# GpSimd takes the first unit's second-level sums in one row, the down-projection folds go two chunks at a time, and VectorE's order at the end of phase 3 changes

## The chip, the cores and the metric

The kernel runs on one core of a Trainium2 chip. Its engines work side by side and wait for one another through semaphores: TensorE (PE in the profile, with its weight loads as PEld), VectorE (DVE), ScalarE (ACT), GpSimd (POOL), and SyncE (SP), which here only issues DMAs. The metric is the device time of one execution in microseconds (us); lower is better.

## The reference

One transformer layer with its two branches in parallel, in float32, on an input of 2 batches x 1024 tokens x 512 features:

```python
xn = layernorm(x)
# linear attention, 16 heads of 32
Q, K, V = elu(xn @ wq.T + bq) + 1, elu(xn @ wk.T + bk) + 1, xn @ wv.T + bv
KV, K_sum = sum_s K[s] V[s]^T, sum_s K[s]                 # for each head
attn = (Q KV / (Q . K_sum + 1e-8)) @ wo.T + bo
# feed-forward, 1376 hidden units, with low-rank terms of rank 8
w = top-2 of 8 experts by sigmoid(xn @ W_router) + bias, normalised scores
gate = xn @ W_gate + (xn @ sA_gate @ sB_gate + sum_e w_e xn @ A_gate[e] @ B_gate[e]) / 8
up   = likewise with W_up, sA_up, sB_up, A_up, B_up
hidden = silu(gate) * up
ffn = hidden @ W_down + (hidden @ sA_down @ sB_down + sum_e w_e hidden @ A_down[e] @ B_down[e]) / 8
out = x + attn + ffn
```

The shared low-rank factors (sA, sB) don't depend on the token, so the kernel adds their product to the weights ("folds" it in); the experts' terms are computed apart.

## The kernel before, in words

All products are done by a scheme of seven products for a 2x2 split (instead of eight), for which sums and differences of blocks of the weights and of the activations have to be made first. Engine order is written out by hand for PE, DVE, ACT and POOL: each runs its instructions in the order in which the program emits them. Only SP's order of DMA issues is chosen by the framework.

Phases 1 and 2 (to about 251 us of the span) normalise and transpose the tokens, make keys and queries, and store the scaled queries to memory. Phase 3 (251 to 532 us) makes the hidden units. Phase 4 (from 532 us) multiplies hidden units and queries with the down and the attention-output weights, in four units.

**Phase 3** consists of ten units `unit(j, b)`: pairs of 128-column weight chunks `j` = 0 to 4, each for batch `b` = 0 and 1. In a unit five of the seven outer products (numbers 1, 6, 2, 5 and 3) are themselves split by the seven-product scheme; each is an `Inner` object with steps `a`, `b`, `c`, `d` of matmuls of 128x256 (line 955) into two PSUM banks tagged `ab0/x0` or `ab1/x1`, copies by ACT (lines 965 to 988) and additions by DVE (`a_sum` line 969, `c_sum` line 983, `d_sum` line 991). Products 7 and 4 are plain 128x512 matmuls (line 1015) into banks `held2/held3`; low-rank terms (line 1010) go there and into `held0/held1`. DVE adds the products up (`add`, line 1037), ACT applies silu (line 1022), and a delayed list (`later`, `flush`) holds the multiplications h*up (line 1025) with their stores to `h_dram`. `unit` has named places (`at("6c")`, `at("1d")` and so on) where the caller hooks other work in.

For an inner product, second-level sums are needed: of the weights (`inner_weight_sums`, lines 930 to 933; `p` names the outer product, 1, 5 and 6 together as 128x384, 2 and 3 alone as 128x128) and of the tokens (`token_sums_56` and `token_sums_23` through line 886 as 128x512, `token_sums_1` lines 908 to 911 as 128x256; four operations each). Weight sums are made for each j, token sums once for each batch. `token_diffs` (line 1251) makes `xdiff0` and `xdiff1`, read by the low-rank matmuls late in every unit. `u4 = r5 + u2` in each unit is two POOL additions of 128x512.

Before the change, DVE makes the token sums of batch 1 and p = 1, 5, 6 inside `unit(0, 0)` and the weight sums of p = 2 just ahead of it; POOL makes `ti23_0` near the end of phase 2, then the weight sums of p = 3, `xdiff`, u4, and `ti23_1`.

**Folding the down weights** (`fold_down`): for each pair of 128-row chunks of `W_down` (`wd[j]`, chunks j and j + 5), two matmuls with 8 rows of contraction (line 1178) multiply the low-rank factors into two banks `x0`, `x1`; DVE adds them to the weights (line 1182, 128x512 each), and POOL makes four block differences (lines 1144 to 1147). The 8 rows lie in one of four groups of 32 partitions, `rows = slice(i % SG * 32, ...)` with i = 8 + chunk and SG = 4. The same is done in the units for the gate and up weights (`fold_pe`, line 716), there with four matmuls of 8x256 at a time. In `unit(4, 0)` and `unit(4, 1)` five such pairs and the rest `wdr` are folded, one pair at a time.

**The end of phase 3**: behind its last `d` step, PE goes straight into phase 4's `products(0, ...)`: for each of seven accumulators two matmuls of 128x256 (line 1383). Those take the banks ab0, ab1, x0, x1, then held0, held1, held2; held0 and held1 are first read out by `add(V, u4, u4, py)`. Chunk n = 1 needs `feature_sums(0, 1)` (lines 1267 to 1270, four operations of 128x256 on DVE) from its third matmul on. The h tiles have three buffers (`hp`, bufs=3), so that the fourth silu of a unit waits for the store of the first h.

Of the kernel before, what the change touches and what calls it, by code (L numbers as in the profile page):

```python
# [37 lines left out]
def layer_kernel(  # L38
# [23 lines left out]
    nc = tc.nc  # L62
# [832 lines left out]

    def token_sums_56(b, t):
        yield from sums_of_four(nc.vector, tsum_pair[b], t)
        inner_tokens(b, (5, 6), lambda i, k: t[:, i, k])
# [4 lines left out]

    def token_sums_1(b):

        t = xnT[b][0][:, :, TB:BT].rearrange("p k (h n) -> p k h n", n=TH)
        b11, b21 = tsum[b][1][:, 0], tsum[b][1][:, 1]
        nc.vector.tensor_sub(t[:, 0, 0], b11[:, TH:], b11[:, 0:TH])
        nc.vector.tensor_sub(t[:, 0, 1], b21[:, TH:], t[:, 0, 0])
        nc.vector.tensor_sub(t[:, 1, 0], b21[:, TH:], b11[:, TH:])  # L910
        nc.vector.tensor_sub(t[:, 1, 1], b21[:, 0:TH], t[:, 0, 1])
        inner_tokens(b, (1,), lambda i, k: t[:, k // 2, k % 2])
# [34 lines left out]
    class Inner:  # L947


        def __init__(self, j, b, p, tag, n):  # L950
            self.w, self.t = WI[j, p], TI[b, p]
            self.n, self.name = n, f"{p}_{tag}"

        def mm(self, out, n, start=False):
            nc.tensor.matmul(out, self.w[n], self.t[n], start=start, stop=True, skip_group_check=True)  # L955

# [43 lines left out]
    def unit(j, b, hooks={}):  # L1000
# [43 lines left out]
        V, G = nc.vector, nc.gpsimd  # L1044
        late_x = b == 1 or j == NP - 1
        pb = [held(f"b{m}_{tag}", 2 + m) for m in range(2)]
# [85 lines left out]
        at("3d")  # L1132
        flush()
        add(V, u4, u4, py)
        r3 = i3.r
        add(V, r3, r3, u4)
# [26 lines left out]

    def fold_down(js, rest=False):

        to, pf = [], []

        def products():
            for j in js:
                for half in range(2):  # L1170
                    to.append((j + half * NP, wd[j][:, 2 * half : 2 * half + 2, :].rearrange("p s n -> p (s n)")))
            if rest:
                to.append((FULL, wdr[0:REST, :]))
            for f, v in to:
                i, n = 2 * NC + f, v.shape[0]
                rows = slice(i % SG * 32, i % SG * 32 + RANK)
                pf.append(spare_bank(f"x{len(pf)}", f"pfd{f}"))
                nc.tensor.matmul(pf[-1][0:n, :], sat[rows, i // SG, 0:n], sb_d[rows, :], start=True, stop=True)

        def sums():  # L1180
            for (f, v), p in zip(to, pf):
                nc.vector.tensor_add(v, v, p[0 : v.shape[0], :])
            for j in js:
                block_diffs(wd[j])
            if rest:
                for t, w in ((wdr_diff, wdr), (bd_diff, bd_sb)):
                    nc.gpsimd.tensor_sub(t, w[:, 0:HD], w[:, HD:D])

        return products, sums
# [34 lines left out]
    denominators(1)  # L1224
    list(token_sums_56(0, slot(6, [2, 4, TH], "ti56_0")))
    rest(0, (fold(0, 0), lambda: attend(1, 0)))
    attend(1, 1)
    list(token_sums_23(0, slot(4, [2, 4, TH], "ti23_0")))
    token_sums_1(0)
    rest(1, (fold(0, 1), lambda: list(inner_weight_sums(nc.vector, 0, (1, 5, 6)))))  # L1230
# [11 lines left out]
    ti56_1 = p3.tile([P, 2, 4, TH], F32, name="ti56_1")  # L1242
    list(inner_weight_sums(nc.vector, 0, (2,)))
    list(inner_weight_sums(nc.gpsimd, 0, (3,)))
    xdiff = []
# [19 lines left out]
    def feature_sums(u, i):  # L1265
# [4 lines left out]
        nc.vector.tensor_sub(t[:, 7, :], t[:, 2, :], t[:, 5, :])  # L1270

    def next_pair(j):

        pf = {}


        free = ("held0", "held1", "x0", "x1"), ("ab0", "x0", "ab1", "x1")

        def pe(i):
            return lambda: pf.update({i: fold_pe(j, i, free[i])})  # L1280

# [22 lines left out]
    for j in range(NP - 1):  # L1304
# [3 lines left out]
        if j == 0:  # L1308
            first["3b"] = [lambda: list(token_sums_23(1, slot(7, [2, 4, TH], "ti23_1")))]
            first["2c"] = [token_diffs]  # L1310
            sums1 = token_sums_56(1, ti56_1)
            for at in ("1d_sum", "6d_sum"):
                first[at] = [lambda: next(sums1, None)] * 2
            first["5b"] = [lambda: token_sums_1(1)]
            first["3d"] = [lambda: next(sums1, None)]
        unit(j, 0, first)
        unit(j, 1, second)
    load_down(1, 8)
    load_down(2, "t3")
    folds = [fold_down((j,)) for j in (1, 2, 0, 3, 4)]  # L1320
    fold_wdr = fold_down((), rest=True)
    unit(NP - 1, 0, {
        "6c": [folds[0][0]], "1d": [folds[0][1]], "5b": [folds[1][0]], "5c": [folds[1][1]],
        "3c": [fold_wdr[0]], "3d": [fold_wdr[1]],
    })
    load_down(0, 6)
    load_down(3, 0)
    load_down(4, 1)
    for i in range(3):
        load_feature(0, i)  # L1330
    unit(NP - 1, 1, {
        "6c": [folds[2][0]], "1d": [folds[2][1]], "2c": [folds[3][0]], "5c": [folds[3][1]],
        "3b": [lambda: feature_sums(0, 0)], "3c": [folds[4][0]], "3d": [folds[4][1]],
        "end": [lambda: feature_sums(0, 1), lambda: feature_sums(0, 2)],
    })
# [190 lines left out]
```

## Time and profile before

| | before |
|---|---|
| device time, median of 3 runs | 756.84 us (755.92 to 757.6) |
| the profiled execution, its own time | 756.2 us |
| its span, first to last instruction | 754.4 us |
| PE busy | 739.2 us (98%), 3106 instructions |
| DVE busy | 470.4 us (62%), 979 instructions |
| ACT busy | 201.1 us (27%) |
| POOL busy | 147.8 us (20%), 189 instructions |
| DMA | 63.29 MB, mean 84 GB/s |
| granted TensorE clock | 0.997 |

The profile shows each engine's busy intervals with the line of the kernel, the operation, its tiles and shapes. "x8" behind a line counts merged instructions, and a float32 matmul appears as two. A bracket at the end tells how long the engine had stood idle before that line, and who ended the wait. Start times count from the start of the span. L955 is line 955 of the kernel before; the changed file is one to six lines off from there.

### The profile page before, as it was taken

The page shows a single profiled execution, that of the slowest core. Times are in us where ns is not written, and L with a number is a line of the kernel's source. Part 1 is how long each engine was busy: PE and PEld are TensorE (multiplying, and loading weights), DVE is VectorE, ACT ScalarE, POOL GpSimd, SP SyncE. Part 2 cuts the span into 40 slices and gives each one's busy share as a digit, 9 for nine tenths or more (in the row PEclk, how much of TensorE's full clock was granted, in tenths as well). Part 3 has the DMA queues.
Part 4 walks back from the last instruction along what each step waited for, and adds up shares of the span by engine and source line. Part 5 has one row for each costly group of instructions (what it writes and reads, how often), then busy time and mean ns, then how long its engine had stood idle before and what let it go on. Part 6 is the DMA issues. An engine that isn't in the chain of part 4 may idle for free.

```text
span 754.4 us, 8739 instructions
## 1 busy us (share of the span) xinstructions
PE 739.2 (98%) x3106; PEld 496.8 (66%) x3106; DVE 470.4 (62%) x979; ACT 201.1 (27%) x432; POOL 147.8 (20%) x189
## 2 busy tenths in 40 slices
PE   8999999999999999999999999999899999999997
PEld 6666666454333566566666666656688888888886
DVE  5666665455677888888888879777942602603303
ACT  3545352533433233333343343333000000000000
POOL 3211212012000541312213114144701002201001
PEclk9999999999999999999999999999999999999999
DMA  8701001007314001211210301353555407312001
GB/s 244 215 28 43 15 0 57 0 1 190 113 29 136 22 4 56 83 53 37 84 57 29 112 29 56 112 167 111 168 161 173 146 10 239 125 60 109 28 1 56
DMA packets 52733, 63.29 MB, mean 84 GB/s; under 512 B 9425, under 2 KB 39505, under 8 KB 52434
## 3 DMA queue, kind: packets, MB, share of 16 engines
q1 hardware_dynamic: 52018, 62.46, 26.0%
q8 instruction: 24, 0.39, 0.2%
q10 hardware_dynamic: 672, 0.28, 0.2%
q14 instruction: 19, 0.16, 0.1%
HBM read 40.97 MB, written 21.76 MB: 83 GB/s over the span
## 4 chain that ended last, share of the span: by engine, by line
PE 83%; DVE 11%; ACT 2%; issue 2%; DMA 1%; POOL 0%; DVEq 0%; SPq 0%; ACTq 0%; POOLq 0%
PE po L1383 24%; PE ab L955 13%; PE pk L279 7%; PE pg L307 6%; PE b L1015 6%; PE pqu L559 3%; PE ph L1406 3%; DVE r L1037 2%; PE x L955 2%; PE pqv L559 2%; PE pxa L638 2%; PE b L1010 2%; PE pr L850 2%; PE x L1010 1%; DVE t L1037 1%
## 5 line engine op out<-in xcount | busy, mean ns | idle before, releaser
L1383 PE MATMUL po<-wd,f 128*128 128x256 f32 x560 | 123.1, 380 | 2.5 <-DVE f L1269 1.2
L1383 PEld LDWEIGHTS po<-wd,f 128*128 128x128 f32 x560 | 105.8, 190 | 19.4 <-issue 2.1
L1015 PE MATMUL b<-t,w 128*128 128x512 f32 x160 | 83.2, 601 | 0.0
L279 PE MATMUL pk<-wk_sb,xnT 128*128 128x256 f32 (+1 forms) x256 | 61.0, 392 | 1.4 <-ACT xnT L267 1.4
L307 PE MATMUL pg<-kt,xn 128*128 128x512 f32 x128 | 57.5, 592 | 0.0
L1413 DVE TENSOR_TENSOR had<-ph,wT 64x256 f32<-64x256 f32 x8 | 3.4, 422 | 86.0 <-PE ph L1406 85.9
L279 PEld LDWEIGHTS pk<-wk_sb,xnT 128*128 128x128 f32 x256 | 48.4, 194 | 9.3 <-ACT xnT L267 2.1
L1430 ACT COPY a<-po 128x512 f32<-128x512 f32 x4 | 2.3, 585 | 195.7 <-PE po L1383 195.7
L1383 PE MATMUL po<-kvo,f 128*128 128x256 f32 x224 | 49.4, 381 | 0.0
L1037 POOL TENSOR_TENSOR r<-r,r 128x512 f32<-128x512 f32 x20 | 30.3, 1537 | 87.7 <-DVE t L1037 87.7
L1383 PEld LDWEIGHTS po<-kvo,f 128*128 128x128 f32 x224 | 42.2, 190 | 7.1 <-issue 1.2
L955 PE MATMUL ab<-ti,wi 128*128 128x256 f32 x180 | 45.7, 380 | 0.0
L955 PEld LDWEIGHTS ab<-ti,w 128*128 128x128 f32 x140 | 25.2, 189 | 30.0 <-DVE r L983 9.1
L955 PEld LDWEIGHTS ab<-ti,wi 128*128 128x128 f32 x180 | 34.1, 190 | 13.9 <-issue 5.3
L955 PE MATMUL ab<-ti,w 128*128 128x256 f32 x140 | 41.1, 387 | 1.1 <-DVE r L983 0.8
L1037 DVE TENSOR_TENSOR r<-r,r 128x512 f32<-128x512 f32 x60 | 41.2, 726 | 0.0
L307 PEld LDWEIGHTS pg<-kt,xn 128*128 128x128 f32 x128 | 24.3, 190 | 25.2 <-issue 23.7
L988 ACT COPY r<-ab 128x256 f32<-128x256 f32 x50 | 18.6, 372 | 76.3 <-PE ab L955 76.3
L1015 PEld LDWEIGHTS b<-t,w 128*128 128x128 f32 x160 | 29.2, 190 | 10.9 <-issue 6.6
L305 POOL TENSOR_TENSOR ksum<-ksum,kt 128x512 f32<-128x512 f32 x14 | 19.9, 1423 | 78.4 <-DVE kt L297 47.7
L983 DVE TENSOR_TENSOR r<-r,ab 128x256 f32<-128x256 f32 x50 | 20.5, 415 | 18.4 <-ACT r L980 17.8
L991 DVE TENSOR_TENSOR r<-r,ab 128x256 f32<-128x256 f32 x50 | 20.8, 417 | 16.9 <-ACT r L988 16.7
(234 smaller groups left out, 1257.7 us busy)
## 6 DMA issues: line engine op xcount, KB each, us to landing
h_dram<-h SPq DMA_DIRECT2D x40, 256.0 KB
f<-h_dram SPq DMA_DIRECT2D x20, 512.0 KB
x_ring<-in_x_dram SPq DMA_DIRECT2D x16, 256.0 KB
q_dram<-qt SPq DMA_DIRECT2D x16, 256.0 KB
f<-q_dram SPq DMA_DIRECT2D x8, 512.0 KB
xr<-in_x_dram SPq DMA_DIRECT2D x8, 512.0 KB
out_dram<-xr SPq DMA_DIRECT2D x16, 256.0 KB
w<-in_w_gate_dram SPq DMA_DIRECT2D x10, 256.0 KB
```

What stands on the lines that cost most here:

```text
L279: nc.tensor.matmul(pk[s], xt(i // TPBATCH, c, cols), wk_sb[:, c, s * HD : (s + 1) * HD + s * E], start=(c == 0), stop=(c == NC - 1),)
L305: nc.gpsimd.tensor_add(ksum, ksum, kt)
L307: nc.tensor.matmul(pg[m], xn[:, ts(m, P)], kt, start=(j == 0), stop=(j == TPBATCH - 1))
L559: nc.tensor.matmul(banks[c], wqs[p][:, k, ts(c, P)], tsum[b][p][:, k, :], start=(start and k == 0), stop=(k == 1), skip_group_check=True,)
L955: nc.tensor.matmul(out, self.w[n], self.t[n], start=start, stop=True, skip_group_check=True)
L983: nc.vector.tensor_add(self.r[1][:, H1], self.r[1][:, H1], self.lo)
L991: nc.vector.tensor_add(self.r[1][:, H0], self.r[1][:, H0], self.lo)
L1010: nc.tensor.matmul(banks[m], bgu_sb[rows, cols], act[rows, :], start=starts[m], stop=True, skip_group_check=True)
L1015: nc.tensor.matmul(pb[m], ws[m][:, A_OF[p], ts(k, P)], tsum[b][p][:, k, :], start=start, stop=True, skip_group_check=True)
L1037: eng.tensor_add(to[m], t[m], v[m])
L1383: nc.tensor.matmul(ps[p][:, q, :], lhsT, rhs, start=start, stop=stop, skip_group_check=True)
L1406: nc.tensor.matmul(ph[g * ER : (g + 1) * ER, :], a, f[:, g, :], start=(n == 0), stop=(n == len(chunks) - 1), skip_group_check=True,)
```

## The change

1. **The first unit's sums.** The DVE operations for the second-level sums of p = 2 weights (j = 0), `ti56_1`, and `token_sums_1` of batch 1 go to POOL, and `ti23_0`, which POOL made in phase 2, moves behind them. All of POOL's sums then stand in one row ahead of unit (0, 0): weights p = 2, weights p = 3, `ti23_0`, `token_sums_1(1)`, `ti56_1`, `ti23_1`, and behind them `xdiff` and u4 of unit (0, 0). An inner product looks its operands up when it emits a matmul, since they are registered later.
2. **Folds of down.** Chunks 1 and 3 are folded together at "6c" of unit (4, 0), chunks 0 and 2 together at "6c" of unit (4, 1), with the banks held0, held1, x0, x1; chunk 4 as before; the rest `wdr` at "6d" of unit (4, 0). Chunk 3 takes the `t3` buffer and chunk 2 the slot that was chunk 3's. In unit (4, 0), `u1 += px` stands behind i5's `c_sum` instead of ahead of i2's `b`.
3. **DVE's order at the end of phase 3.** In unit (4, 1) the two delayed h multiplications no longer stand ahead of `u4 += py`, but behind the feature sums; `feature_sums(0, 1)` comes between `u4 += py` and `r3 += u4`.

On SP one order changes: the second load for chunk 4 goes behind two h stores of unit (4, 0).

```diff
@@ -893,22 +893,22 @@
             TI[b, p] = {1: raw[:, 0, 0:TH], 2: raw[:, 1, 0:TH], 3: raw[:, 1, TH:TB],
                         4: t(i, 3), 5: t(i, 0), 6: t(i, 1), 7: t(i, 2)}
 
-    def token_sums_56(b, t):
-        yield from sums_of_four(nc.vector, tsum_pair[b], t)
+    def token_sums_56(eng, b, t):
+        yield from sums_of_four(eng, tsum_pair[b], t)
         inner_tokens(b, (5, 6), lambda i, k: t[:, i, k])
 
     def token_sums_23(b, t):
         yield from sums_of_four(nc.gpsimd, xnT[b][1].rearrange("p k (g n) -> p g k n", g=2), t)
         inner_tokens(b, (2, 3), lambda i, k: t[:, i, k])
 
-    def token_sums_1(b):
+    def token_sums_1(eng, b):
 
         t = xnT[b][0][:, :, TB:BT].rearrange("p k (h n) -> p k h n", n=TH)
         b11, b21 = tsum[b][1][:, 0], tsum[b][1][:, 1]
-        nc.vector.tensor_sub(t[:, 0, 0], b11[:, TH:], b11[:, 0:TH])
-        nc.vector.tensor_sub(t[:, 0, 1], b21[:, TH:], t[:, 0, 0])
-        nc.vector.tensor_sub(t[:, 1, 0], b21[:, TH:], b11[:, TH:])
-        nc.vector.tensor_sub(t[:, 1, 1], b21[:, 0:TH], t[:, 0, 1])
+        eng.tensor_sub(t[:, 0, 0], b11[:, TH:], b11[:, 0:TH])
+        eng.tensor_sub(t[:, 0, 1], b21[:, TH:], t[:, 0, 0])
+        eng.tensor_sub(t[:, 1, 0], b21[:, TH:], b11[:, TH:])
+        eng.tensor_sub(t[:, 1, 1], b21[:, 0:TH], t[:, 0, 1])
         inner_tokens(b, (1,), lambda i, k: t[:, k // 2, k % 2])
 
     WI = {}
@@ -948,11 +948,12 @@
 
 
         def __init__(self, j, b, p, tag, n):
-            self.w, self.t = WI[j, p], TI[b, p]
+            self.of = (j, p), (b, p)
             self.n, self.name = n, f"{p}_{tag}"
 
         def mm(self, out, n, start=False):
-            nc.tensor.matmul(out, self.w[n], self.t[n], start=start, stop=True, skip_group_check=True)
+            w, t = WI[self.of[0]][n], TI[self.of[1]][n]
+            nc.tensor.matmul(out, w, t, start=start, stop=True, skip_group_check=True)
 
         def a(self):
             self.r = [u_tile(f"r{m}_{self.name}") for m in range(2)]
@@ -1042,7 +1043,7 @@
 
         i1, i6, i2, i5, i3 = (Inner(j, b, p, tag, i + b) for i, p in enumerate((1, 6, 2, 5, 3)))
         V, G = nc.vector, nc.gpsimd
-        late_x = b == 1 or j == NP - 1
+        late_x = b == 1
         pb = [held(f"b{m}_{tag}", 2 + m) for m in range(2)]
         i1.a()
         activate()
@@ -1130,8 +1131,10 @@
         i3.d()
         i3.d_sum()
         at("3d")
-        flush()
+        if (j, b) != (NP - 1, NBATCH - 1):
+            flush()
         add(V, u4, u4, py)
+        at("w")
         r3 = i3.r
         add(V, r3, r3, u4)
         hidden(0, 1, r3)
@@ -1161,7 +1164,7 @@
             )
         wd[j] = t
 
-    def fold_down(js, rest=False):
+    def fold_down(js, at, rest=False):
 
         to, pf = [], []
 
@@ -1174,7 +1177,7 @@
             for f, v in to:
                 i, n = 2 * NC + f, v.shape[0]
                 rows = slice(i % SG * 32, i % SG * 32 + RANK)
-                pf.append(spare_bank(f"x{len(pf)}", f"pfd{f}"))
+                pf.append(spare_bank(at[len(pf)], f"pfd{f}"))
                 nc.tensor.matmul(pf[-1][0:n, :], sat[rows, i // SG, 0:n], sb_d[rows, :], start=True, stop=True)
 
         def sums():
@@ -1222,11 +1225,10 @@
     low_rank_in(2)
     low_rank_in(3)
     denominators(1)
-    list(token_sums_56(0, slot(6, [2, 4, TH], "ti56_0")))
+    list(token_sums_56(nc.vector, 0, slot(6, [2, 4, TH], "ti56_0")))
     rest(0, (fold(0, 0), lambda: attend(1, 0)))
     attend(1, 1)
-    list(token_sums_23(0, slot(4, [2, 4, TH], "ti23_0")))
-    token_sums_1(0)
+    token_sums_1(nc.vector, 0)
     rest(1, (fold(0, 1), lambda: list(inner_weight_sums(nc.vector, 0, (1, 5, 6)))))
     flush()
     ps8.close()
@@ -1240,8 +1242,12 @@
     hp = pool(ph3, "hp", bufs=3)
     p3 = pool(ph3, "p3")
     ti56_1 = p3.tile([P, 2, 4, TH], F32, name="ti56_1")
-    list(inner_weight_sums(nc.vector, 0, (2,)))
-    list(inner_weight_sums(nc.gpsimd, 0, (3,)))
+    for p in (2, 3):
+        list(inner_weight_sums(nc.gpsimd, 0, (p,)))
+    list(token_sums_23(0, slot(4, [2, 4, TH], "ti23_0")))
+    token_sums_1(nc.gpsimd, 1)
+    list(token_sums_56(nc.gpsimd, 1, ti56_1))
+    list(token_sums_23(1, slot(7, [2, 4, TH], "ti23_1")))
     xdiff = []
     for b in range(NBATCH):
         xdiff.append(ffn.tile([P, TB], F32, tag="den" if b == 0 else "xd", name=f"xdiff{b}"))
@@ -1269,15 +1275,16 @@
         nc.vector.tensor_sub(t[:, 5, :], t[:, 4, :], t[:, 0, :])
         nc.vector.tensor_sub(t[:, 7, :], t[:, 2, :], t[:, 5, :])
 
+
+    FREE = ("held0", "held1", "x0", "x1"), ("ab0", "x0", "ab1", "x1")
+
     def next_pair(j):
 
         pf = {}
 
 
-        free = ("held0", "held1", "x0", "x1"), ("ab0", "x0", "ab1", "x1")
-
         def pe(i):
-            return lambda: pf.update({i: fold_pe(j, i, free[i])})
+            return lambda: pf.update({i: fold_pe(j, i, FREE[i])})
 
         def adds(i):
             return lambda: fold_adds(j, i, pf.pop(i))
@@ -1306,32 +1313,25 @@
             load_weights(j + 1)
         first, second = next_pair(j + 1)
         if j == 0:
-            first["3b"] = [lambda: list(token_sums_23(1, slot(7, [2, 4, TH], "ti23_1")))]
             first["2c"] = [token_diffs]
-            sums1 = token_sums_56(1, ti56_1)
-            for at in ("1d_sum", "6d_sum"):
-                first[at] = [lambda: next(sums1, None)] * 2
-            first["5b"] = [lambda: token_sums_1(1)]
-            first["3d"] = [lambda: next(sums1, None)]
         unit(j, 0, first)
         unit(j, 1, second)
     load_down(1, 8)
-    load_down(2, "t3")
-    folds = [fold_down((j,)) for j in (1, 2, 0, 3, 4)]
-    fold_wdr = fold_down((), rest=True)
-    unit(NP - 1, 0, {
-        "6c": [folds[0][0]], "1d": [folds[0][1]], "5b": [folds[1][0]], "5c": [folds[1][1]],
-        "3c": [fold_wdr[0]], "3d": [fold_wdr[1]],
-    })
+    load_down(3, "t3")
+    folds = [
+        fold_down((1, 3), FREE[0]), fold_down((), ("x1",), rest=True), fold_down((0, 2), FREE[0]),
+        fold_down((4,), ("x0", "x1")),
+    ]
+    unit(NP - 1, 0, {"6c": [folds[0][0]], "1d": [folds[0][1]], "6d": [folds[1][0]], "7": [folds[1][1]]})
     load_down(0, 6)
-    load_down(3, 0)
+    load_down(2, 0)
     load_down(4, 1)
     for i in range(3):
         load_feature(0, i)
     unit(NP - 1, 1, {
-        "6c": [folds[2][0]], "1d": [folds[2][1]], "2c": [folds[3][0]], "5c": [folds[3][1]],
-        "3b": [lambda: feature_sums(0, 0)], "3c": [folds[4][0]], "3d": [folds[4][1]],
-        "end": [lambda: feature_sums(0, 1), lambda: feature_sums(0, 2)],
+        "6c": [folds[2][0]], "1d": [folds[2][1]],
+        "3b": [lambda: feature_sums(0, 0)], "3c": [folds[3][0]], "3d": [folds[3][1]],
+        "w": [lambda: feature_sums(0, 1)], "end": [lambda: feature_sums(0, 2), flush],
     })
     activate()
     activate()
```

## The prediction

> **What bounds the kernel now.** First the page's busy times:
>
> ```profile
> PE 739.2 (98%) x3106; PEld 496.8 (66%) x3106; DVE 470.4 (62%) x979; ACT 201.1 (27%) x432; POOL 147.8 (20%) x189
> ```
>
> PE is busy nearly throughout, so only two things shorten the kernel: PE work that goes away, and the few gaps. The list of what PE waited for has no entry above 1.8 us in total, so next I read PE's timeline where the change acts, and looked for idle brackets and for rows longer than their like.
>
> ```profile
> 256.97 1.79 PE L716 MATMUL pf<-sb,sat 8*128 8x256 f32 x8
> ...
> 263.39 0.71 PE L716 MATMUL pf<-sb,sat 8*128 8x256 f32 x8
> ...
> 287.29 0.70 PE L955 MATMUL ab<-xnT,w 128*128 128x256 f32 x2 [1.04 <-DVE r L983]
> ...
> 531.58 0.70 PE L955 MATMUL ab<-ti,w 128*128 128x256 f32 x2 [0.57 <-DVE r L983]
> ...
> 537.46 3.69 PE L1383 MATMUL po<-wd,f 128*128 128x256 f32 x16 [0.92 <-DVE r L1037]
> 542.33 8.04 PE L1383 MATMUL po<-wd,f 128*128 128x256 f32 x36 [1.17 <-DVE f L1269]
> ```
>
> The first two rows are the same four matmuls; the first takes 1.08 us more, since it waits for banks. The others wait for DVE. The chain of waits from 528 to 546 us (start, duration, what) shows what DVE was doing:
>
> ```profile
> 533.57 1.20 DVE wd L1182 x2
> 534.76 1.96 DVE h L1025 x2
> 536.72 2.96 DVE r L1037 x4
> 539.68 0.87 DVE f L1267
> 540.55 0.86 DVE f L1268
> 541.41 0.88 DVE f L1269
> ```
>
> Phase 4's start hangs on DVE alone: the h multiplications (1.96) stand ahead of the additions that free held0. Third, POOL and DVE beside each other in the first unit (start, duration):
>
> ```profile
> 277.78 1.26 POOL L886 TENSOR_TENSOR ti<-xnT 128x512 f32<-128x512 f32 x1
> ...
> 281.57 1.72 POOL L886 TENSOR_TENSOR ti<-xnT,ti 128x512 f32<-128x512 f32 x1
> ...
> 278.40 1.28 DVE L1037 TENSOR_TENSOR r<-r,b 128x512 f32<-128x512 f32 x2 [0.30 <-PE b L1010]
> ...
> 282.10 1.75 DVE L1025 TENSOR_TENSOR h<-h,t 128x512 f32<-128x512 f32 x1
> ```
>
> A POOL sum of 512 elements takes 1.26 us, beside DVE 1.6 to 1.7. DVE's r<-r,b (one operand from PSUM) is not slowed at 278.40 although POOL is busy; h<-h,t (both from SBUF) takes 1.75 instead of the 0.68 it takes elsewhere.
>
> **What the Trainium skill says.** "SBUF — State Buffer", section "SBUF: two separate sides": GpSimd and a VectorE instruction with two SBUF inputs exclude each other for a whole instruction. The rows above agree in kind, with overlap at the edges. "TensorEngine Tiling (Array Packing)", section "Key Properties": row tiles work in parallel. The trace agrees: four folds of 8x256 in different row groups take 0.65 us (263.39 to 264.04), where one after another they would take 4 x 0.43. "GPSIMD Engine Reference", section 3.1: a two-input float32 addition of 2048 is 1.96 times slower than on DVE; here, at 512, 1.26 against 0.68 us is 1.85.
>
> **Part 1, POOL's row.** DVE loses 12 operations: weights p = 2 (1.35 + 3 x 0.28, though only 0.21 from start to start), `ti56_1` 4 x 0.68, `token_sums_1` 4 x 0.42: 6.6 us. What it gives PE: `a_sum` (257.27 to 258.0 now, behind the weights of p = 2) runs at about 255 us, so the fold matmuls of 256.97 no longer wait for x0 and x1, gaining 1.0. At the unit's end DVE's h multiplications (281.0 to 283.85 beside POOL) run clear and gain 1.2, so the 1.04 gap at 287.29 mostly goes as well.
>
> What it costs is POOL's time. The weights of p = 2 need only the last fold addition (247.97 us), not the four sums behind it. From 248.0: 8 weight sums of 128 elements beside DVE at 0.77 (the 250.24 row and its followers) are 6.2, to 254.2; `ti23_0` 4 x 1.24, to 259.2 (PE needs it at 266.7); `token_sums_1` 4 x 0.70 (pace of the block differences at 509.8), to 262.0; `ti56_1`, two alone and two beside u2's additions, 2 x 1.25 + 2 x 1.65, to 267.8; `ti23_1` 3 x 1.25 + 1.65, to 273.2; the first `xdiff` 1.65, to 274.9. Its matmul stands at 277.17 now, at about 276.3 then: 1.4 us of reserve. u4 follows to about 279.5 (277.8 now); u2 += pb waits for it, which I put at 279.2 to 279.5 against 278.4 now, and i3's `c_sum` stands at about 279.15 against 278.1. So DVE additions with two SBUF operands get slower here (u2, r2, t: two each, some 0.7 us apiece, 4 us), and in mid-unit PE gives the gained 1.0 back; by 287.29 the two shortenings win. Net **-0.9**. Bounds: -2.0 (both gaps closed whole) to +3 (each POOL sum at its contended duration, below).
>
> **Part 2, folds.** Chunks 1 and 3 are chunks 1, 6, 3, 8, i = 9, 14, 11, 16: four different row groups; 0 and 2 likewise (8, 13, 10, 15). Two 8x512 fold matmuls take 1.06 us now (487.65, 518.58); four should take the same 1.06, as the 8x256 ones do. So two slots of 1.06 fall away, one in each unit. If they didn't overlap, they would cost 2.1 and the gain would be nothing; I take the overlap.
> - Unit (4, 0): -1.06 for the slot at 487.65, -0.2 for the rest's wait at 497.48. The rest is moved, not removed (1.0 both times). Against that, POOL now takes differences of two chunks and the rest's from about 479.7 to 487, beside DVE's two h and two u2 additions (some +0.3 each), and `wdr` (0.68) is ahead of them: t[0] is ready at about 489.35, where PE wants it at 489.0: +0.3. Net **-0.95**.
> - Unit (4, 1): -0.3 (wait at 507.88, DVE having lost `wdr` at 502.33 and the `h` row's contention), -1.06 (slot at 518.58), -0.57 (gap at 531.58: with POOL's differences done by 516, u4 starts at about 523.5 instead of 527.0 and no longer meets the feature sums that took 1.15 + 1.48 instead of 2 x 0.42). Net **-1.9**.
>
> The loads are no limit: chunk 3 comes in the place where chunk 2's load stood (issued by 472.1, DMA quiet from 476.5, addition at 479.7), chunk 2 at 479.6, chunk 4's second half behind two h stores at about 504, needed after 525. The four banks are free where the gate folds use the same four, at "6c".
>
> **Part 3, DVE at the end.** Relative to PE's last `d` step (531.58 now; call it 529.65 with part 2's gain in this unit): `d_sum` +1.57, 0.42; two fold additions 1.20; then directly u4 += py, whose first frees held0 at about 533.5. PE's first eight po matmuls end at about 534.3: no wait, against 1.4 us of pause before 537.46. `feature_sums(0, 1)` begin at 534.05, beside POOL's differences 0.87 each; the third is done at 536.7. PE needs it after six more matmuls (2.6) and two (0.87), at 537.8: no wait, against 1.4 us before 542.33. From first po matmul to n = 1's third: 9.8 us now, 7.2 then. Net **-2.6**.
>
> What is late next: r3 += u4 to 539.5, feature sums of n = 2 to 543.1 (third needed at 543.7, done 542.2), then the h multiplications. The fourth silu waits for the first h's store, now issued at about 544.0 instead of 535.6. I let the store take 2.5 us, because the loads that now lie ahead of it (4 us of transfers at 532.8 to 541) are over; then silu 0.63, multiplication 0.68, and feature sums of n = 3, third done at 549.0; PE needs it at 549.7. All SP instructions behind that store (hr, xr) come about 1 us later than now and are needed 10 us on. From there PE shows no gap to the end (543 to 566, 566 to 580 and 700 to 740 us are 100% busy), so the gain stays.
>
> **Sum.** -0.9 - 0.95 - 1.9 - 2.6 = -6.35. The profiled execution took 756.2 (span 754.4): 749.85 (span 748.05). The median of the runs stands 0.64 above the profiled one: **750.5**.
>
> **Rivals.**
> - A, POOL's row is late: contended durations for half of it make `xdiff` and u4 2 to 3 us later; part 1 is +1.5 instead of -0.9, 752.9. For it: all POOL sums in the unit stand ahead of `xdiff`, and a wait of 1.4 us is all the reserve. Against: DVE from 254 to 264.8 has only PSUM operations.
> - B, the fourth silu: the store takes the 5.1 us it takes now (535.62 to 540.74). Then DVE stands before that multiplication and n = 3 waits 2 us: 752.5. Against: the transfers ahead of it.
> - C, slower: the row at contended durations throughout: 8 x 0.95 + 4 x 1.7 + 4 x 1.2 + 8 x 1.7 + 1.65 = 34.5 us from 248.0, `xdiff` at 282.5, PE stalled 6.2; u4 at 286 then holds up DVE's next `a_sum`, and another 2 us. Part 1 is +8 and the whole +2.5: 759.4. It decides from a first `xdiff` later than about 281.5. Against: 26 POOL operations would have to meet a two-SBUF addition each, and DVE has some 20 of them in this window.
> - D, four folds don't overlap: +2.1, 752.6. Against: the 0.65 us above.
>
> **Chances.** Forecast 0.60 (749.0 to 751.8), A 0.15, B 0.07, D 0.05, C 0.09, no change (mishaps that cancel) 0.04. Range 748.9 to 754.0, which takes in A, B and D with most of their widths and part 1's lower bound. A measurement can tell about 0.2% (1.5 us) from no change: faster 0.86, same 0.05, slower 0.09.
>
> **What would show it.** Right: the fold row near 257 at 0.7 us; no gap over 0.3 near 287; rows of eight pfd matmuls of about 1.1 us; no bracket at the first rows of po. Wrong: a wait of PE for `xdiff` or of DVE for u4 near 277 to 285; a wait for i2's `b` on POOL near 266; po at n = 3 waiting for DVE, with ACT waiting for an h store.

## The result and the profile after

The changed kernel takes 748.25 us (median of 5 runs, 746.78 to 749.32) against 756.84 (755.92 to 757.6): a ratio of 0.9888, 95% interval 0.987 to 0.9905, so 7.2 to 9.8 us less. The forecast was 750.5, its range began at 748.9: the sign and every step's direction held, the gain was put 2 us too small. A second set of runs on another chip (the experiment e11_after_again below) gave 747.85 us, ratio 0.989 (0.9873 to 0.9908).

First the busy times of the page after. PE is busy for 5.5 us less with the same 3106 instructions, so its rows got shorter and none fell away; DVE is busy for 4.7 less with 12 instructions fewer, GpSimd for 11.3 more:

```profile
PE 733.7 (98%) x3106; PEld 494.8 (66%) x3106; DVE 465.7 (63%) x967; ACT 201.0 (27%) x432; POOL 159.1 (21%) x201
```

Then PE's timeline after, the rows that answer to those shown of before (start, duration, what; a bracket would be idle time):

```profile
255.74 0.71 PE L716 MATMUL pf<-sb,sat 8*128 8x256 f32 x8
261.08 0.71 PE L716 MATMUL pf<-sb,sat 8*128 8x256 f32 x8
...
284.25 0.70 PE L956 MATMUL ab<-xnT,w 128*128 128x256 f32 x2
...
474.20 1.28 PE L1181 MATMUL pfd<-sb_d,sat 8*128 8x512 f32 x8
...
502.96 1.14 PE L1181 MATMUL pfd<-sb_d,sat 8*128 8x512 f32 x8
...
524.83 0.70 PE L956 MATMUL ab<-ti,w 128*128 128x256 f32 x2
525.36 0.60 PE L956 MATMUL ab<-xnT,w 128*128 128x256 f32 x2
525.79 30.76 PE L1383 MATMUL po<-wd,f 128*128 128x256 f32 x140
```

The first fold row is as short as the second. The 1.04 bracket at 287.29 has gone (284.25), the 0.57 at 531.58 too (524.83). Eight fold matmul records (four matmuls, since a float32 matmul leaves two records) take 1.28 and 1.14 us, where four records took 1.13 to 1.39. Phase 4 runs from 525.79 as one row without a bracket, where it stopped twice.

DVE's timeline at that place shows why. In the chain of waits phase 4 hung on DVE for 7.8 us (533.57 to 541.41 and on); now `u4 += py` stands directly behind the fold's additions. Its first half frees held0 at about 528.6, and PE's ninth po matmul, the first that needs that bank, starts at 529.6:

```profile
526.74 1.28 DVE L1185 TENSOR_TENSOR wd<-wd,pfd 128x512 f32<-128x512 f32 x2
527.93 1.28 DVE L1038 TENSOR_TENSOR r<-r,y 128x512 f32<-128x512 f32 x2
529.13 0.94 DVE L1273 TENSOR_TENSOR f<-f 128x256 f32<-128x256 f32 x1
...
542.62 0.69 DVE L1026 TENSOR_TENSOR h<-h,r 128x512 f32<-128x512 f32 x1 [2.42 <-ACT h L1023]
```

The last row is rival B's place: DVE does stand before the fourth multiplication, for 2.42 us, since ACT waits for the first h's store. That store took about 3.0 us, not 5.1; the third feature sum of n = 3 is done at 544.3, and PE comes to the matmul that needs it, its 45th of po, at 545.2. So PE doesn't wait, by 0.9 us.

To place the time, cut both profiled executions into five stretches at the same PE rows: the fold row near 257, the first pfd row of each of the last two units, the first po row, the end. Lengths in us; the forecast's steps are sorted into the same stretches ((4, 0) -0.95 and the 0.3 of the wait at 507.88 into the third row).

| stretch | before | after | change | forecast | e11_after_again |
|---|---|---|---|---|---|
| start to the fold row | 256.97 | 255.74 | -1.23 | 0 | 257.09 |
| to the first pfd row (part 1) | 220.27 | 218.46 | -1.81 | -0.9 | 218.44 |
| to unit (4, 1)'s pfd row (part 2) | 30.64 | 28.76 | -1.88 | -1.25 | 28.76 |
| to the first po row (part 2) | 24.66 | 22.83 | -1.83 | -1.63 | 22.82 |
| to the end (part 3) | 221.86 | 219.21 | -2.65 | -2.6 | 219.59 |
| span | 754.4 | 745.0 | -9.4 | -6.4 | 746.7 |

The first stretch isn't the change's doing. PE's first rows with a weight from memory, the before kernel's first:

```profile
8.02 4.58 PE L279 MATMUL pk<-wk_sb,xnT 128*128 128x256 f32 x12 [0.84 <-ACT xnT L267]
```

and the changed kernel's:

```profile
8.21 2.90 PE L279 MATMUL pk<-wk_sb,xnT 128*128 128x256 f32 x12 [0.84 <-ACT xnT L267]
```

This code is the same in both. What differs is the granted TensorE clock: from 9 to 12 us of the span it is 0.50 in the profile of before and 1.00 in that of the changed kernel, and behind 8.9 us the row's records start every 0.43 us in the first and every 0.22 us in the second. Over the profiled executions of this case the row takes 2.90 to 5.57 us, and it shifts everything behind it: the first stretch is 255.74 to 258.81 us long. In e11_after_again, the changed kernel once more, the clock was 0.50 there again, the row took 4.58, the first stretch 257.09, and the span was 746.7. The three middle stretches repeat to 0.02 us. The last one doesn't (219.21 and 219.59): in e11_after_again PE waits another 0.40 us at 637.41 for an addition of the output, far from the change. So what follows compares stretches, and uses the timed ratios as the check on them. What the change brings is -7.8 to -8.2 by stretches, -8.5 and -8.3 by times.

### The profile page after: what moved, and what is told of

The parts are those of the page before. It is cut to its first block, busy times and chain, and to the rows that moved or that the text cites. A ratio compares the mean times of both kernels' runs of the same rounds, so it can differ in the third digit from the quotient of the medians.

```text
span 745.0 us, 8741 instructions
## 1 busy us (share of the span) xinstructions
PE 733.7 (98%) x3106; PEld 494.8 (66%) x3106; DVE 465.7 (63%) x967; ACT 201.0 (27%) x432; POOL 159.1 (21%) x201
## 4 chain that ended last, share of the span: by engine, by line
PE 87%; DVE 8%; ACT 2%; issue 1%; DMA 0%; POOL 0%; DVEq 0%; ACTq 0%
PE po L1383 25%; PE ab L956 15%; PE b L1016 7%; PE pk L279 7%; PE pg L307 6%; PE pqu L559 3%; PE ph L1406 3%; PE x L956 2%; PE pqv L559 2%; PE pxa L638 2%; PE pr L850 2%; PE b L1011 2%; DVE r L1038 2%; PE x L1011 1%; PE pv L355 1%
## 5 line engine op out<-in xcount | busy, mean ns | idle before, releaser
L279 PE MATMUL pk<-wk_sb,xnT 128*128 128x256 f32 (+1 forms) x256 | 59.3, 384 | 1.4 <-ACT xnT L267 1.4
L1038 DVE TENSOR_TENSOR r<-r,r 128x512 f32<-128x512 f32 x60 | 44.1, 776 | 0.0
L989 ACT COPY r<-ab 128x256 f32<-128x256 f32 x50 | 18.6, 372 | 71.8 <-PE ab L956 71.8
L966 ACT COPY r<-ab 128x256 f32<-128x256 f32 x50 | 18.6, 373 | 49.1 <-PE ab L956 46.9
L984 DVE TENSOR_TENSOR r<-r,ab 128x256 f32<-128x256 f32 x50 | 20.9, 418 | 17.2 <-ACT r L981 16.7
```

The source lines that it names most:

```text
L279: nc.tensor.matmul(pk[s], xt(i // TPBATCH, c, cols), wk_sb[:, c, s * HD : (s + 1) * HD + s * E], start=(c == 0), stop=(c == NC - 1),)
L966: nc.scalar.copy(self.r[0][:, H0], self.ua)
L984: nc.vector.tensor_add(self.r[1][:, H1], self.r[1][:, H1], self.lo)
L1038: eng.tensor_add(to[m], t[m], v[m])
```

## The experiments

T1 is the theory read from the table: the three parts add up, each at the size of its stretch.

**Each part alone.** Part 1 alone is the kernel before with GpSimd's row (and the late look-up of `WI` and `TI` that it needs):

```
-    list(token_sums_23(0, ...));  token_sums_1(0)          # rest(1)
-    list(inner_weight_sums(nc.vector, 0, (2,)))
-    list(inner_weight_sums(nc.gpsimd, 0, (3,)))
+    token_sums_1(nc.vector, 0)
+    for p in (2, 3): list(inner_weight_sums(nc.gpsimd, 0, (p,)))
+    list(token_sums_23(0, ...));  token_sums_1(nc.gpsimd, 1)
+    list(token_sums_56(nc.gpsimd, 1, ti56_1));  list(token_sums_23(1, ...))
```

> Part 1 alone (POOL's row of sums; folds and the end of phase 3 as before). Theory T1 (read from the changed kernel's trace: PE never gives the gained 1.0 us back, and both shortened places add up): -1.8 us, with the fold row near 257 us at 0.7 us, the gap of 1.04 us near 287 gone, and no other part of phase 3 shorter. The prediction's own reading (PE gives the 1.0 us back in mid-unit): -0.9 us. Rival: part 1's gain is only passed on because later parts shorten the end too, and DVE's pauses at phase 4's start take it back: 0 us.

Measured: 754.71 us, ratio 0.998 (0.9973 to 0.9987), so -1.5 (-2.0 to -1.0). Its second stretch is 218.50, -1.77 as T1 said (-1.8); all others but the first are those of before.

Part 2 alone: `folds` and its hooks of the two last units, the loads, and `late_x = b == 1`.

> Part 2 alone (chunks 1 with 3 and 0 with 2, the rest at another place). T1: -3.7 us, -1.5 in unit (4, 0) and -2.2 in unit (4, 1), and both pauses of PE at phase 4's start (before rows of po) stay at about 1.4 us. The prediction's: -2.85. Rival (an earlier PE only waits longer for DVE at phase 4's start): -1 or less, with longer pauses there.

Measured: 752.53 us, ratio 0.9949 (0.9937 to 0.9962), -3.9 (-4.8 to -2.9). Second stretch 220.27 (unchanged), third 28.76, fourth 22.83: the changed kernel's to 0.01, -3.7 together as T1 said. Both pauses at phase 4's start stay (brackets of 0.92 and 1.17 us), so an earlier PE does not wait longer there.

Part 3 alone: `flush` and the features of n = 1 at the end of unit (4, 1).

> Part 3 alone (h multiplications and feature sums in another order at the end of the last unit of phase 3). T1: -2.9 us, both pauses at phase 4's start gone, nothing else changed. The prediction's: -2.6. Rival (with the chunk pairs folded one after another POOL's differences still slow DVE, so the feature sums are late): -1.5, one pause left.

Measured: 753.81 us, ratio 0.9971 (0.996 to 0.9982), -2.2 (-3.0 to -1.4). PE's timeline of this kernel, its first po row:

```profile
532.18 30.11 PE L1385 MATMUL po<-wd,f 128*128 128x256 f32 x137
```

Both pauses are gone, and the other gaps of before are still there. Its last stretch is 219.52 (-2.34), where T1 said -2.9. Phase 4's first unit alone (first po row to the second unit's first) shrinks from 56.26 to 53.66 us, -2.60, here and in both profiles of the changed kernel; the rest to the end varies with a wait of 0.2 to 0.6 us in all for the output's additions. The four stretches of the three kernels sum to -1.77 - 1.88 - 1.83 - 2.34 = -7.82, e11_after_again's sum and 0.35 from the first profile's: within that, the parts are additive, none covers or uncovers another.

**Do four folds overlap because they sit in four row groups?** The changed kernel with chunks paired so that two of the four folds share a group of 32 rows:

```
-    fold_down((1, 3), FREE[0]), ..., fold_down((0, 2), FREE[0]),
+    fold_down((1, 2), FREE[0]), ..., fold_down((0, 3), FREE[0]),
```

> The changed kernel with other pairs: chunks 1 and 2, then 0 and 3, so that in each slot of four fold matmuls two lie in the same group of 32 rows (groups 1, 2, 2, 3 and 0, 1, 3, 0 instead of four different ones); nothing else changes. Theory that the gain comes from row groups working side by side: each slot 0.9 to 1.0 us longer (about 2.0 instead of 1.1), +1.9 us against the changed kernel, so -6.5 against before. Rival (any four small matmuls in a row cost the same; the gain is only the saved switches between large and small matmuls): 0 against the changed kernel, -8.4 against before.

Measured: 750.45 us, ratio 0.9927 (0.9915 to 0.994), -5.5 against before, some 3 more than the changed kernel; by stretches +1.23 and +0.83, so +2.1. PE's timeline, where four folds took 1.28:

```profile
477.14 1.99 PE L1181 MATMUL pfd<-sb_d,sat 8*128 8x512 f32 x8
```

So the overlap is there, and it comes from the row groups: with two in one group the row takes 0.71 and 0.84 more, and a rule by which any four small matmuls cost the same is out. That is rival D's mechanism. That it costs the +2.1 said of D is in part luck: the two rows are 1.5 of it, and the other 0.5 is PE's wait for DVE's `t` at 490.04 (below, under part 2).

**How near was a late row (rivals A and C)?** The changed kernel with the last sum of `ti23_1` made again, the same values, ahead of the first `xdiff`: twice, and six times.

```
+    for _ in range(2):          # 6 in the second kernel
+        nc.gpsimd.tensor_sub(ti23_1[:, :, 3], b21, ti23_1[:, :, 1])
     xdiff = []
```

> The changed kernel with two more 128x512 sums in GpSimd's row, directly ahead of the first xdiff (the last sum of ti23_1 made again, the same values). Changed kernel: about -8.4 against the kernel before. T1 (PE reaches the xdiff matmuls 0.75 us after the first xdiff is there, and nothing later gives lost PE time back): the sums take 1.25 to 1.65 us each, so xdiff comes 2.5 to 3.3 us later and PE waits 1.8 to 2.5 us at the xdiff matmuls; +2.2 us against the changed kernel, -6.2 against before. The prediction's reserve of 1.4 us: +1.4, -7.0. Rival (the unit hides a late row behind DVE's idle time): +0.5 at most, -7.9.

> The changed kernel with six more 128x512 sums in GpSimd's row ahead of the first xdiff. T1: 7.5 to 9.0 us later, less 0.75 of reserve; PE waits once, for xdiff, and the two additions of u4 follow directly, so the u4 wait is hidden behind the same pause: +7.3 us against the changed kernel, -1.1 against before. The prediction's rival C (a late u4 costs another 2 us at DVE's next additions): +9.3, so +0.9 against before, which would be slower than before. Rival (given back later in the unit): +5 or less.

Measured with two: 750.81 us, ratio 0.9925 (0.9912 to 0.9938), -5.7 against before; second stretch +2.44 against the changed kernel. PE's timeline:

```profile
278.88 1.13 PE L1011 MATMUL b<-xdiff,bgu_sb 64*128 64x512 f32 x4 [2.62 <-POOL xdiff L1261]
```

The two sums took 3.28 us, PE waited 2.62 (2.70 by the rows' starts) and later saved the 0.24 it had waited for DVE. The reserve at `xdiff` was thus about 0.7 us (3.28 - 2.62; in the changed kernel's own trace the first `xdiff` ends 0.7 us ahead of its matmul), not the 1.4 of the prediction, and behind it a late row costs all it is late by. T1 holds (+2.2 said).

With six: 757.42 us, ratio 1.0012 (1.0002 to 1.0023), +0.9 against before: about as much slower as the whole change had made it faster. Second stretch +8.94, where T1 said 7.3. PE's timeline:

```profile
283.59 2.08 PE L1011 MATMUL b<-xdiff,bgu_sb 64*128 64x512 f32 x4 [7.85 <-POOL xdiff L1261]
285.45 1.89 PE L1011 MATMUL y<-xa,bgu_sb 64*128 64x512 f32 x4
```

and the stretches of this kernel (width, busy time of PE, PEld, DVE, ACT and POOL, granted TensorE clock, DMA share, GB/s):

```profile
275.50:283.50 8.00, 0.24 (x2) 0.00 (x0) 2.33 (x3) 0.89 (x2) 7.69 (x7) 0.80 0.00 0
283.50:285.40 1.90, 1.81 (x4) 0.85 (x6) 0.00 (x0) 0.00 (x0) 1.90 (x3) 0.50 0.00 0
285.40:287.20 1.80, 1.80 (x6) 0.34 (x2) 0.69 (x1) 0.00 (x0) 1.79 (x2) 0.50 0.00 0
287.20:290.00 2.80, 2.80 (x13) 2.04 (x12) 1.84 (x4) 1.27 (x3) 0.00 (x0) 1.00 0.00 0
```

The wait is 7.85 (7.92 by the rows' starts), then the matmuls run at half the granted clock for 3.7 us: the two rows take 2.08 and 1.89 where they took 1.13 and 1.02, and from the first one's start to the next row it is 3.68 us instead of two times 0.96, 1.76 more. Against that PE saves some 0.75 of small waits behind it: 7.92 + 1.76 - 0.75 = 8.93. Rival C's price (+9.3) was met by luck, since its second term was named wrongly. DVE does wait for u4 (8.17 us, at 286.00), but no row of PE behind it waits for DVE; the second term is PE's clock after a long pause. The Trainium skill says this in "TensorE: Matmul & The Clock Gate", Part 1 (The HAM clock gate), section "What's actually happening": the array runs at half rate after an idle window of about 3.4 us and at the full rate again after about as long a busy one. The traces here agree: no slow row after 2.62 us of pause, slow ones after 3.58 (below) and 7.85. Worked out from the granted clock of the stretches, it was halved for about 3.4 us after the pause of 3.58, and for about 6.9 us at the pause of 7.85, of which 3.2 lay within the pause.

**Why did PE not give the 1.0 back in mid-unit?** Two DVE sums, a value made early and again, put directly behind `t += r5` of the first unit, in the kernel before and in the changed one (`b21` stands for the sum's own operand):

```
         add(V, t, t, r5)
+        if (j, b) == (0, 0):
+            for _ in range(2):
+                nc.vector.tensor_sub(ti56_1[:, :, 3], b21, ti56_1[:, :, 1])
```

> The kernel before, with two more 128x512 sums on DVE in the first unit, directly behind t += r5 (the last sum of ti56_1, made early and again). They delay i3's a_sum and c_sum by 1.3 us, or by up to 2.8 beside GpSimd's u4. T1 (DVE stands idle 1.9 us ahead of c_sum, and c_sum is done 1.0 us before PE's i3.d wants it, so additions that get slower here are hidden up to that size): +0.0 to +0.4 us. The prediction's step (a c_sum that comes 1.05 later takes 1.0 from PE): +1.0 to +2.0.

> The changed kernel with the same two DVE sums at the same place. T1 (the slower additions beside GpSimd have used up that idle time: PE already waits 0.24 us for c_sum): the whole delay lands on PE, +2.5 us against the changed kernel (2.4 to 3.0 for two sums beside u4), -5.9 against before. Rival (there is still idle time as in the kernel before): +0.4, -8.0.

In the kernel before: 757.26 us, ratio 1.0012 (1.0005 to 1.0018), +0.9 (0.4 to 1.4); second stretch +0.88. The sums took 3.43 beside u4, and `c_sum` was done 1.35 later than before. PE's timeline of this kernel, the two places where it now waits:

```profile
280.53 0.70 PE L955 MATMUL ab<-ti,w 128*128 128x256 f32 x2 [0.37 <-DVE r L983]
...
289.20 0.70 PE L955 MATMUL ab<-xnT,w 128*128 128x256 f32 x2 [1.50 <-DVE r L983]
```

DVE's `a_sum` ahead of `c_sum` came 3.3 us later, the idle time took up 1.9 of that, and of the 1.35 left at `c_sum` only 0.4 reached PE in mid-unit. The other 0.47 is the gap at the next unit's start, which grew from 1.04 to 1.50: the h multiplications start 0.4 us later, and the first takes 1.63 us beside GpSimd instead of 1.18. T1 (0 to 0.4) holds for mid-unit and missed that second place.

In the changed kernel: 753.3 us, ratio 0.9957 (0.9943 to 0.9971), -3.3 against before, so about 5 more than the changed kernel; second stretch +4.59, where T1 said 2.5. PE's timeline:

```profile
283.31 0.70 PE L956 MATMUL ab<-ti,w 128*128 128x256 f32 x2 [3.58 <-DVE r L984]
...
286.01 1.84 PE L1016 MATMUL b<-t,w 128*128 128x512 f32 x2
```

and its stretches, in the columns explained above:

```profile
283.30:285.20 1.90, 1.89 (x7) 1.58 (x8) 1.40 (x3) 0.37 (x1) 0.00 (x0) 0.75 0.00 0
285.20:287.60 2.40, 2.40 (x5) 1.31 (x4) 2.40 (x5) 0.90 (x2) 0.00 (x0) 0.50 0.28 95
```

The sums' 3.41 us land on PE whole (+3.3): no cover is left, as T1 said. The remainder is the half clock again (1.84 for a row of 1.02; 1.6 us in all, of which PE saves 0.4 later), which T1 had not reckoned with.

**The order at the end.** The changed kernel with the two h multiplications back ahead of `u4 += py`, the features of n = 1 left where the change put them:

```
-        if (j, b) != (NP - 1, NBATCH - 1):
-            flush()
+        flush()
...
-        "w": [...feature_sums(0, 1)], "end": [...feature_sums(0, 2), flush],
+        "w": [...feature_sums(0, 1)], "end": [...feature_sums(0, 2)],
```

> The changed kernel with the two h multiplications of the last unit back ahead of u4 += py; the feature sums of n = 1 stay ahead of r3 += u4. T1: u4 += py, which frees held0, is 1.4 to 2.0 us later (529.3 to 530.7 us), PE has run its eight po matmuls by 529.3 and waits about 1.4; the feature sums that follow stay behind PE: +1.4 us against the changed kernel, -7.0 against before. Rival (the feature sums, not the order of the h multiplications, were what counted): +0.3. Rival (both pauses come back): +2.9.

Measured: 749.16 us, ratio 0.9899 (0.9886 to 0.9912), -7.6 against before; last stretch 220.88, +1.3 to +1.7 against the two profiles of the changed kernel. PE's timeline:

```profile
526.82 4.00 PE L1382 MATMUL po<-wd,f 128*128 128x256 f32 x16
531.74 27.00 PE L1382 MATMUL po<-wd,f 128*128 128x256 f32 x124 [0.92 <-DVE r L1038]
```

The first pause is back, the second isn't. Phase 4's first unit takes 54.81 us here, 53.66 in the changed kernel and 56.26 before: so the order of the h multiplications is worth 1.15 us (T1 said 1.4), and the place of the feature sums the other 1.45. Each half of part 3 removed one pause. The times alone (-7.6 against -8.3 and -8.5) don't separate this kernel from the changed one; the pause in the row does.

**One step further.** If a slot of PE's costs more than the folds in it, the remainder's fold can go into chunk 4's slot, a third matmul in a third row group. Its addition to `wdr` stands on DVE ahead of `u2 += pb`, its differences on GpSimd behind chunk 4's:

```
-    fold_down((1, 3), ...), fold_down((), ("x1",), rest=True), fold_down((0, 2), ...),
-    fold_down((4,), ("x0", "x1")),
+    fold_down((1, 3), ...), fold_down((0, 2), ...),
+    fold_down((4,), ("x0", "x1", "ab0"), rest=True),
```

> The changed kernel with the remainder's fold put beside the two of chunk 4, as a third matmul in a third row group with bank ab0, its addition to wdr on DVE ahead of u2 += pb and its differences on GpSimd behind chunk 4's. T1 (a slot of its own costs PE about 1 us, a third fold in a free row group next to nothing; DVE has 1 us of idle time ahead of i3's d_sum): -1.0 us against the changed kernel, -9.4 against before. Rival (the addition to wdr pushes u4 += py back and PE waits at its ninth po matmul): -0.4. Rival (the third fold costs as much here as alone): 0.

> The changed kernel once more, beside the one with the remainder's fold in chunk 4's slot, so that the two stand on one chip: -8.4 us against the kernel before. Its first weights' matmuls (4.58 us in the profile of before, 2.90 in the first profile of the changed kernel) vary from run to run, and its span with them: 745.0 plus up to 2.5 us.

> The changed kernel with the remainder's fold beside chunk 4's, once more: T1 (a slot of PE's less) -1.0 us against the changed kernel run beside it, -9.4 against before. Rival (no gain): 0.

Measured: 747.28 us, ratio 0.9875 (0.9862 to 0.9888); again, beside the changed kernel, 747.78, ratio 0.9883 (0.9861 to 0.9906), where the changed kernel had 747.85 and 0.989 (0.9873 to 0.9908). PE's timeline of the first, three folds in one row:

```profile
522.22 1.13 PE L1181 MATMUL pfd<-sb_d,sat 8*128 8x512 f32 x6
```

The third stretch is 27.74 and 27.73 where it was 28.76, the others stay: 1.02 us less of PE's time, twice, as T1 said. That is just the length of the slot itself (480.11 to 481.13 in the changed kernel), and the third fold costs next to nothing beside the other two (1.13 us for the row, as with two). The times lie on that side both times, with intervals that overlap the changed kernel's, so by time alone the gain isn't shown. By its stretches it is the shortest kernel of this study, by one part in seven hundred.

## Why the prediction was wrong by 2 us

The bound (PE, and the gaps where it waits for DVE), the steps and their signs held, and the sum was 1.8 us short of the change's own effect in the first profile (1.4 in e11_after_again). By its steps:

- **Part 1, "in mid-unit PE gives the gained 1.0 back": failed, 0.9 us.** This is the step that made the forecast wrong. The fold row gave 1.08 as said, and the end of the unit (from the row behind i3's `d` on) 0.86 (0.9 said). In between PE lost only 0.13, or 0.3 at `c_sum` less the 0.20 us of a wait at 270.54 that went. The contention itself was sized rightly: GpSimd's and DVE's timelines of the changed kernel show `xdiff` at 272.25, which is 273.5 with the first stretch's 1.23 put back (273.2 said), and DVE's u2, r2 and t in 2.48, 2.37 and 3.10 where they take 1.28 each, 4.1 in all (4 said).

```profile
272.25 3.39 POOL L1257 TENSOR_TENSOR xdiff<-xa 128x512 f32<-128x512 f32 x2
275.60 2.95 POOL L1038 TENSOR_TENSOR r<-r,r 128x512 f32<-128x512 f32 x2
```

```profile
273.09 3.10 DVE L1038 TENSOR_TENSOR t<-t,r 128x512 f32<-128x512 f32 x2
276.11 0.41 DVE L970 TENSOR_TENSOR r<-r,x 128x256 f32<-128x256 f32 x1
276.44 0.41 DVE L984 TENSOR_TENSOR r<-r,ab 128x256 f32<-128x256 f32 x1
277.35 0.69 DVE L1038 TENSOR_TENSOR r<-r,b 128x512 f32<-128x512 f32 x1 [0.49 <-POOL r L1038]
```

What failed is where the 4 us end: the prediction let i3's `c_sum` end 1.05 us later (279.15 against 278.1). It ended at 276.85, which is 278.08 with the shift: no later at all. DVE's timeline of the kernel before has a bracket just there:

```profile
275.38 0.41 DVE L969 TENSOR_TENSOR r<-r,x 128x256 f32<-128x256 f32 x1
277.68 0.42 DVE L983 TENSOR_TENSOR r<-r,ab 128x256 f32<-128x256 f32 x1 [1.89 <-ACT r L980]
```

  The four `token_sums_1` that DVE lost and its earlier start with PE took up some 2 of the 4 us, so that `a_sum`, the row ahead of `c_sum`, ran 1.96 us later than before (276.11 + 1.23 against 275.38); and there DVE had stood idle for 1.89 us. PE in turn came 1.26 us earlier than before to a `c_sum` that had been done 1.0 us ahead of it (278.10, wanted at 279.09), and waited for the difference:

```profile
276.91 0.70 PE L956 MATMUL ab<-ti,w 128*128 128x256 f32 x2 [0.24 <-DVE r L984]
```

  e9_dve_before measured that cover (1.35 late, 0.4 paid), and e10_dve_after that the change has spent it: in the changed kernel the same sums are paid whole. The prediction gives no working for its 1.05, so which part of the cover it left out stays open.
- **Part 2, the slot "of 1.06": mis-sized, 0.4 us.** PE's timelines before and after, the same place in unit (4, 0):

```profile
485.83 1.89 PE L955 MATMUL ab<-ti,wi 128*128 128x256 f32 x8
487.65 1.13 PE L1178 MATMUL pfd<-sb_d,sat 8*128 8x512 f32 x4
488.71 0.70 PE L955 MATMUL ab<-ti,wi 128*128 128x256 f32 x2
489.24 1.02 PE L1015 MATMUL b<-t,w 128*128 128x512 f32 x2
```

```profile
483.82 2.32 PE L956 MATMUL ab<-ti,wi 128*128 128x256 f32 x10
485.98 1.02 PE L1016 MATMUL b<-t,w 128*128 128x512 f32 x2
```

  From the row of 485.83 to the row of 489.24 before is 3.41 us, and the same ten matmul records in the changed kernel take 2.16: taking the slot away saved 1.25. In unit (4, 1), from the same row to the one behind the `b` matmul (516.33 to 520.60 before, 511.43 to 514.44 after), it was 1.26. The difference from 1.06 is about 0.1 us ahead of the fold and 0.1 behind it (0.70 for a row of 0.59), at each change of matmul shape, which my sum left out. That four folds cost what two do held, and e4_clash showed why.
- **Part 2, "t[0] ... +0.3": failed, 0.3 us.** The contention was expected on DVE and fell on GpSimd, which holds nothing up here. Its timeline and then DVE's, in the changed kernel:

```profile
482.00 2.92 POOL L1190 TENSOR_TENSOR wdr_diff<-wdr 97x256 f32<-97x256 f32 x1
484.89 0.72 POOL L1190 TENSOR_TENSOR bd_diff<-bd_sb 128x256 f32<-128x256 f32 x1
```

```profile
481.85 1.28 DVE L1026 TENSOR_TENSOR h<-h,r 128x512 f32<-128x512 f32 x2
483.05 1.28 DVE L1038 TENSOR_TENSOR r<-r,r 128x512 f32<-128x512 f32 x2
```

  Four DVE operations with two SBUF inputs ran one behind the other at their full speed, and a GpSimd operation that is no larger than the next one's 0.72 took 2.92, until 0.6 us past the end of the last. It is 2.92 in e2, e5, e7, e10 and e11 too. In e4_clash, where GpSimd stood idle for 0.83 us ahead of the same operation, the two engines took turns instead: the four DVE operations took 3.64 instead of 2.56, GpSimd 1.12, `t` came late, and PE lost the prediction's step after all (0.5 us). So the step was possible, and that it didn't come is in part luck; what decides between the two isn't shown.
- **Part 2's waits: right, each a little small.** -0.27 for the rest's (0.2 said), -0.37 at (4, 1)'s fold (0.3). The rest of unit (4, 1) comes to -0.57, the number said, but by luck: the gap before i3's `d` gave 0.64 and the last fold row with its neighbours 0.36, and a new wait for DVE at 515.19 with what follows took 0.43 back. The gap didn't go for the reason given either: u4 still met the feature sums, which took 1.16 and 1.48. They began 1.6 us earlier relative to PE, because a fold addition of 1.28 us no longer stood ahead of them and the additions r and t took 1.29 each instead of 1.82 and 2.02.
- **Part 3: right.** -2.60 in phase 4's first unit in every profile that has it, -2.6 said; each half removed its pause (e7_flush).
- **Rivals.** A and C were nearer than written: the reserve at `xdiff` was 0.7 us, not 1.4 (e5_late2), PE having come 0.4 earlier than said and `xdiff` 0.3 later, and DVE did wait for u4, 0.49 and 0.55, without PE waiting. C's price was right and its second term wrong (e6_late6). B's mechanism is in the trace, with the store at 3.0 where 2.5 was let and 5.1 was feared. D is excluded.
- **The range.** Its lower end took in part 1's bound of -2.0 but let the other steps stand at their values; several small terms in part 2 were all rounded against the gain, which the range didn't allow for.

## What to carry to other kernels

When work on a helper engine slows a second engine, follow the delay to the engine that sets the end and subtract on the way what the second engine no longer has to do and every idle bracket: 4 us of slower additions here cost PE 0.3 us at `c_sum`, where PE had shown no gap before. After such a change the cover is spent, and the next microsecond at that place is paid whole. A slot between matmuls of one shape costs more than its own matmuls (1.25 for 1.06 here; one beside a row of another shape cost its own 1.02), so small matmuls belong together in one slot, in different row groups. And compare two profiles by stretches behind the first microseconds, where the granted clock can differ from one execution to the next.

## What the runs showed of the hardware

- Four fold matmuls of 8x512 in four row groups: 1.14 and 1.28 us a row, as two (1.13 to 1.39) and three (1.13); with two of four in the same group 1.98 and 1.99.
- GpSimd against DVE, two SBUF inputs each: in the first unit they took turns (GpSimd 1.7 instead of 1.26, DVE about 1.2 to 1.8 instead of 0.68), but at 482 us GpSimd waited through four DVE operations in a row (2.92 for 0.72). The Trainium skill, "SBUF — State Buffer", section "SBUF: two separate sides", has the lock and that the first to start takes it for its whole instruction, which both fit; that one engine can keep it over several instructions was not expected.
- A PE pause of 2.62 us left the clock at full speed; pauses of 3.58 and 7.85 us were each followed by matmuls at half speed for 3.4 to 3.7 us, which cost 1.6 and 1.8 us more.
- The first row with weights from memory took 2.90 to 5.57 us in the profiled executions, with the same code: 2.90 where the granted clock was 1.00 throughout, 4.58 in before and e11 where it was 0.50 from 9 to 12 us. The first stretch moves with it (255.74 to 258.81 us), which is most of what separates the two profiles of the changed kernel (spans of 745.0 and 746.7).
